# Decoder layer, fp32, one core: where the feed-forward's side work stands in program order

## The chip, the core and the metric

The kernel runs on one core of a Trainium2 chip. The metric is device time in microseconds of one execution. Inside the core, five engines work from queues of their own, each in program order, and meet at semaphores: TensorE (PE; its weight loads are listed as PEld) multiplies matrices, VectorE (DVE) and ScalarE (ACT) work on rows of 128 partitions, GpSimd (POOL) does the same more slowly, SyncE (SP) issues transfers. A profile shows DMA queues (SP's and POOL's are the ones that matter here) whose transfers share 16 DMA engines.

## The reference, cut to what matters

Eight sequences of 256 tokens, width 512, all in float32. One decoder layer with three sublayers, each followed by a layer norm without scale and shift:

```python
x = _layernorm(x + attn(x))                  # 16 heads, low-rank maps folded into the weights
x = _layernorm(x + xattn(x, ctx, ctx, decay))  # q * recurrence over ctx * ctx
gate = jnp.einsum('bsh,ih->bsi', x, gate_w)  # 2048 x 512, a cubic spline through 8134 control points
up   = jnp.einsum('bsh,ih->bsi', x, up_w)
x = _layernorm(x + jnp.einsum('bsi,hi->bsh', silu(gate) * up, down_w))
```

The three weight matrices of the feed-forward are samples of splines, so each row is a smooth curve with few knots. The kernel uses that: it never forms the matrices. It multiplies a 64-row summary of the input for each tile of 128 hidden units.

## The kernel before, in words

Tokens are handled in `NG` = 4 groups of 512, hidden units in `NTILE` = 16 tiles of 128. Attention, the recurrence and the first two norms take the first 400 us of the span; the change does not touch them. What follows is the feed-forward, group by group (`for b in range(NG)`, line 940). One group is:

- *Pairs* (`gate_up`, line 842, for j = 0 to 7). Each pair makes two hidden tiles. The two gates `pg` go to two buffers of the PSUM pool `ps_mm` (4 buffers), the two `pu` to two of `ps_big` (4 buffers); each product uses 64 of the 128 rows of the array, so two run side by side. ACT applies SiLU (`sg`), VectorE multiplies (`inter`).
- *Gathers* (`gather`, line 858). Each `inter` is copied by DMA, 256 KB, into a re-sorted tile `nat`. All 16 gathers are issued on SP.
- *Exact parts* (`exact`, line 865, for t = 0 to 15). Four products of 32 rows each per tile accumulate into the four `y` of the group, which take all four `ps_big` buffers.
- *Sums* (`into_sums`, line 875), four of them, after the eighth exact part. Each multiplies from `nat`, in a `ps_mm` buffer (`ps_s`), is copied to `sum` and moved by DMA into the tile `fin`.
- *Finish* (`finish`, line 894). Four pairs of products from `fin` close the four `y`, and ACT and VectorE copy them to `ys`.

Two other strands are woven in.

*The inputs of the group after* (`inputs(b + 1)`, line 700, run while b is 1 or 2; those of groups 0 and 1 are made during attention). It is a generator of eight units. Units 0 to 3 transpose the normalised rows `x2` (four 128x128 transposes each into a `ps_mm` buffer, `tr_x`), copy them to `x2T` (ACT and VectorE in turn) and write them to DRAM (`xd`: one large transfer on POOL's queue per unit, and from the second unit on a few single rows on SP's). Units 4 to 7 form the *moments*: two products each (`ps_mom`, three `ps_mm` buffers in all); after the second and the last, copies to `mom`, and at the end two writes to DRAM on POOL's queue (`md`). The reads back into `xg` (`windows`, line 683, four transfers behind one more small write; `moments`, line 694, two transfers) are kept in a list `reads` and issued on SP after the last pair.

*The results of the group before* (`outcome(b - 1, t)`, line 907, t = 0 to 3). Four transposes of `ys` into a `ps_mm` buffer (`tr_y`); VectorE adds the residual `x2p` and sums the rows (`h3`, `s3`); then `norm_plain` (line 366): the mean's negative `nm` (VectorE), the square with its row sum (ACT, whose elementwise output goes to `o`), variance and power −1/2 (POOL: `va`, `rs`), the normalised rows (VectorE, to `o`); last the output DMA on SP. `h3` and `o` come from the pool `rows` (6 buffers). A third generator, `residual(b)`, copies `x2` into `x2p` on POOL.

The order of every engine is the program's order: `Ordered` (line 299) pins it. Generators are advanced by two functions. `slot()` (line 348) takes every chain in `chains` one `yield` further; `fill(n)` (line 354) takes n units of the inputs and calls `slot()` after every second one. So the loop at line 940 decides what stands between what: in groups 1 and 2 one unit of the inputs follows each pair, and one more result is begun after each of the first four exact parts. Behind the last group, four results are begun one per `slot()`, and `settle()` runs the chains out.

Of the kernel before, what the change touches and what calls it, by code (L numbers as in the profile page):

```python
# [10 lines left out]
F32 = mybir.dt.float32  # L11
U32 = mybir.dt.uint32
AF = mybir.ActivationFunctionType
# [4 lines left out]
P = 128  # L18
B, T, D = 8, 256, 512
NH, DH = 16, 32  # L20
NT = B * T
DC = D // P
# [4 lines left out]
NG = NT // GT  # L27
TC = GT // P
# [287 lines left out]
def decoder_kernel(ctx: ExitStack, tc: tile.TileContext, x, xT, ctxT, wq, wkT, wvT, woT, wdownT, wup, decay, up_taps, down_taps, mom_f, sum_f, out, plan):  # L316
    nc = tc.nc
# [5 lines left out]
    rows = ctx.enter_context(tc.tile_pool(name="rows", bufs=6, side="left"))  # L323
# [21 lines left out]
    nc = Ordered(tc)  # L345
    units, chains = [], []

    def slot():

        for c in list(chains):  # L350
            if next(c, c) is c:
                chains.remove(c)

    def fill(n):

        for i in range(n):
            if units:
                next(units[0][1])
                units[0][2] -= 1
                if not units[0][2]:  # L360
                    units.pop(0)
            if i % 2:
                slot()
                some_taps()

    def norm_plain(h, s, o):

        nm = small.tile([P, 1], F32, tag="nm", name="nm")
        nc.vector.tensor_scalar(nm, s, -1.0 / D, None, ALU.mult)
        yield  # L370
        ss = small.tile([P, 1], F32, tag="ss", name="ss")
        nc.scalar.activation(o, h, AF.Square, bias=nm, accum_out=ss)
        yield
        va = small.tile([P, 1], F32, tag="va", name="va")
        nc.gpsimd.tensor_scalar(va, ss, 1.0 / D, EPS, ALU.mult, ALU.add)
        rs = small.tile([P, 1], F32, tag="rs", name="rs")
        nc.gpsimd.tensor_tensor(rs, va, neghalf[:, 0:1], ALU.pow)
        yield
        nc.vector.tensor_scalar(o, h, nm, rs, ALU.add, ALU.mult)
# [61 lines left out]
    def some_taps():  # L441
        made[0] += 0.62
        while made[0] >= 1:
            made[0] -= 1
            next(weights, None)
# [237 lines left out]
    def windows(xd, xt, xg):  # L683


        past = SPAN * ND - D
        nc.sync.dma_start(out=xd[4 * (SPAN - past) + 3 :: 4, :], in_=xt[:past, 0, :])
        for h, odd, n, j0 in ((0, 0, NTILE // 2 - 1, 1), (1, NTILE - 1, NTILE // 2 - 1, 0)):
            for t, m, j in ((odd, 1, odd // 2), (2 * j0 + h, n, j0)):
                step = 4 * (lows[t + 2][0] - lows[t][0]) if m > 1 else 0  # L690
                from_ = bass.AP(xd.tensor, xd.offset + 4 * lows[t][0] * GT, [[GT, RAW], [step * GT, m], [1, GT]])
                nc.sync.dma_start(out=xg[h * K2 : h * K2 + RAW, j : j + m, :], in_=from_)

    def moments(md, xg):
        for h in range(2):
            to = h * K2 + RAW
            from_ = bass.AP(md.tensor, md.offset + h * GT, [[NTILE * GT, 20], [2 * GT, NTILE // 2], [1, GT]])
            nc.sync.dma_start(out=xg[to : to + 20], in_=from_)

    def inputs(b):  # L700

        pool, mf = ffn["pool"], ffn["mf"]
        xt = pool.tile([P, DC, GT], F32, tag="x2T", name="x2T")
        xd = ffn["dram"].tile([4 * SPAN, GT], F32, tag="xd", name="xd")
        md = ffn["dram"].tile([1, 20 * NTILE, GT], F32, tag="md", name="md")
        xg = pool.tile([P, NTILE // 2, GT], F32, tag="xg", name="xg", bufs=2)
        xgs[b] = xg
        for c in range(DC):
            tr = ps_mm.tile([P, GT], F32, tag="mm", name="tr_x2")
            for t in range(TC):  # L710
                nc.tensor.transpose(tr[:, t * P : (t + 1) * P], x2[:, b * TC + t, c * P : (c + 1) * P], ident)
            (nc.vector.tensor_copy if c % 2 else nc.scalar.copy)(xt[:, c, :], tr)
            nc.gpsimd.dma_start(out=xd[c : 4 * (P - 1 - c) + c + 1 : 4, :], in_=xt[c:, c, :])
            if c:
                row = 4 * (SPAN - c) + c - 1
                nc.sync.dma_start(out=xd[row : row + 4 * c - 3 : 4, :], in_=xt[:c, c, :])
            yield
        if b > 1:
            reads.append(lambda: windows(xd, xt, xg))
        else:  # L720
            windows(xd, xt, xg)
        mo = ffn["mom"].tile([P, ND, GT], F32, tag="fin", name="mom")
        ps = {}
        for c in range(DC):
            for s in (c, c + 1):
                if s // 2 not in ps:
                    ps[s // 2] = ps_mm.tile([P, GT], F32, tag="mm", name="ps_mom")
                at = slice(s % 2 * K2, (s % 2 + 1) * K2)
                nc.tensor.matmul(
                    ps[s // 2][at, :],  # L730
                    lhsT=mf[:, c, s - c, :],
                    rhs=xt[:, c, :],
                    start=(s == c + 1 or c == 0),
                    stop=(s == c or c == DC - 1),
                )
            if c == 1:
                nc.vector.tensor_copy(mo[:, 0, :], ps[0])
            if c == DC - 1:
                nc.vector.tensor_copy(mo[:, 1, :], ps[1])
                nc.scalar.copy(mo[:K2, 2, :], ps[2][:K2, :])  # L740
                nc.gpsimd.dma_start(out=md[:, : 2 * P].rearrange("h (c p) t -> (h p) c t", p=P), in_=mo[:, :2, :])
                nc.gpsimd.dma_start(out=md[0, 2 * P :], in_=mo[:K2, 2, :])
                if b > 1:
                    reads.append(lambda: moments(md, xg))
                else:
                    moments(md, xg)
            yield
# [4 lines left out]
    for s, (g, bb, quad) in enumerate(steps):  # L752
# [8 lines left out]
        if quad == 0 and n:  # L761
            load_rows(n - 1)
            o = [["o", output(n - 1, qc), DC] for qc in range(2)]
# [43 lines left out]
        if quad % 2:  # L807
            tr = ps_mm.tile([P, 2, T], F32, tag="mm", name="tr_rec")
# [49 lines left out]
    def gather(b, t):  # L858

        g, r = t // NSUM, t % NSUM  # L860
        if not r:
            nats[b, g] = work.tile([P, NSUM, GT], F32, tag=f"nat{g}", name="nat", bufs=1)
        nc.sync.dma_start(out=nats[b, g][r::NSUM], in_=inters[b, t])

    def exact(b, t):

        if t == 0:
            ys[b] = [ps_big.tile([P, GT], F32, tag="big", name=f"y{d}") for d in range(ND)]
        for d in range(ND):
            q = slice(d * 32, (d + 1) * 32)  # L870
            nc.tensor.matmul(
                ys[b][d], lhsT=wd[q, t * P : (t + 1) * P], rhs=inters[b, t][q, :], start=(t == 0), stop=False
            )
# [33 lines left out]
    def outcome(b, t):  # L907

        tr = ps_mm.tile([P, D], F32, tag="mm", name="tr_y")
        for d in range(ND):  # L910
            nc.tensor.transpose(tr[:, d * P : (d + 1) * P], ys[b][:, d, t * P : (t + 1) * P], ident)
        yield
        h3 = rows.tile([P, D], F32, tag="row", name="h3")
        s3 = small.tile([P, 1], F32, tag="s3", name="s3")
        nc.vector.scalar_tensor_tensor(h3, tr, 1.0, xps[b][:, t, :], ALU.mult, ALU.add, accum_out=s3)
        o = rows.tile([P, D], F32, tag="row", name="o")
        yield from norm_plain(h3, s3, o)
        r0 = (b * TC + t) * P
        nc.sync.dma_start(out=out[r0 : r0 + P, :], in_=o)

    def residual(b):

# [17 lines left out]
    for b in range(NG):  # L940
        if 0 < b < NG - 1:
            units.append(["i", inputs(b + 1), 2 * DC])
        for j in range(NTILE // 2):
            gate_up(b, j)
            gather(b, 2 * j)
            gather(b, 2 * j + 1)
            if b:
                slot()
                fill(1)
        if b == 0:  # L950
            fill(2 * DC)
        while reads:
            reads.pop(0)()
        for t in range(NTILE):
            exact(b, t)
            if b and t < TC:
                chains.append(outcome(b - 1, t))
            slot()
            if b == 0 and t < 5:
                slot()  # L960
            if b == 0 and t == 4:
                settle()
                done.close()
                late = ffn["mom"] = ctx.enter_context(tc.tile_pool(name="late", bufs=1, side="right"))
            if t == 7:
                settle()
                chains.append(residual(b))
                for v in range(NSUM // 2):
                    into_sums(b, v)
        assert not units  # L970
        finish(b)
    for t in range(TC):
        chains.append(outcome(NG - 1, t))
        slot()
    settle()
    mid.close()

# [50 lines left out]
```

## Time and profile before

Three runs took 611.3, 610.93 and 611.07 us, median 611.07. The profiled execution took 612.27 us; its span is 610.5 us, and mean granted TensorE clock 0.993 of full speed.

| stage (us from the span's start) | length | PE busy | DVE busy | ACT busy | POOL busy | DMA share |
|---|---|---|---|---|---|---|
| group 1, 449.56 to 501.35 | 51.79 | 50.24 | 20.82 | 16.05 | 14.88 | 0.77 |
| group 2, 501.35 to 555.36 | 54.01 | 51.94 | 20.86 | 16.04 | 14.89 | 0.74 |
| group 3, 555.36 to 598.89 | 43.53 | 43.53 | 18.48 | 14.95 | 11.36 | 0.62 |
| tail, 598.89 to 610.5 | 11.61 | 1.93 | 6.09 | 3.22 | 3.26 | 0.24 |

How to read it: all engines' operations are recorded by one helper (line 308), so groups of instructions are told apart by tile names (`y<-fin` is a product whose operand comes from `fin`). Busy time of TensorE includes the drain of pipelined products. A timeline line gives start, length, engine, operation, output and inputs, shape, count, and in brackets the idle time before it with what ended that. The chain of waits follows the last instruction back to what released it. The DMA share is the mean busy share of the 16 DMA engines, and can read a little over 1. A granted clock of 0.5 means that TensorE ran at half speed.

### The profile page before, as it was taken

How to read it: one execution, taken by the hardware profiler on the slowest of the kernel's cores; microseconds unless marked ns; L12 is line 12 of the kernel's file. 1: busy time of each engine (PE TensorE's matmuls, PEld its weight loads, DVE VectorE, ACT ScalarE, POOL GpSimd, SP SyncE). 2: the span in 40 equal slices, each digit the busy share in tenths (PEclk: the TensorE clock that was granted, in tenths of full speed). 3: DMA queues.
4: the chain of work that ended last, by engine and by line, in shares of the span. 5: the costliest groups of instructions: out<-in, count | busy, mean ns of one | idle time of the engine just before them, and what ended most of it. 6: DMA issues, size and time to landing. Idle time of an engine off the chain costs nothing.

```text
span 610.5 us, 9688 instructions
## 1 busy us (share of the span) xinstructions
PE 584.3 (96%) x3346; PEld 288.8 (47%) x3346; DVE 334.5 (55%) x742; ACT 276.9 (45%) x820; POOL 210.1 (34%) x479
## 2 busy tenths in 40 slices
PE   8999999998999999999999898899999989999993
PEld 3544555555455555555556455444343333334432
DVE  0204545657875666786665778867635316504614
ACT  0115634647555456565556666664233214304402
POOL 0001986264636334644420301202511611350152
PEclk9999999999999999999999999999999999998998
DMA  8104253044124114314101653588129849973931
GB/s 301 52 0 155 89 182 92 20 139 138 53 68 141 35 53 160 118 52 139 47 23 53 176 141 108 156 195 177 71 71 246 226 121 236 222 208 79 217 119 69
DMA packets 39984, 75.50 MB, mean 124 GB/s; under 512 B 3936, under 2 KB 8288, under 8 KB 39936
## 3 DMA queue, kind: packets, MB, share of 16 engines
q1 hardware_dynamic: 36880, 66.94, 40.1%
q0 software_dynamic: 2048, 6.77, 3.4%
q10 hardware_dynamic: 1008, 1.18, 0.6%
q8 instruction: 26, 0.43, 0.3%
q14 instruction: 22, 0.18, 0.1%
HBM read 42.86 MB, written 11.04 MB: 88 GB/s over the span
## 4 chain that ended last, share of the span: by engine, by line
PE 72%; DVE 10%; issue 7%; DMA 5%; ACT 3%; POOL 2%; SPq 0%; POOLq 0%; DVEq 0%; ACTq 0%
PE ps_k L308 9%; PE ps_v L308 9%; PE ps_o L308 8%; PE y L308 8%; PE ps_q L308 7%; PE tr_e L308 6%; PE sc L308 5%; PE av L308 5%; PE pg L308 4%; PE pu L308 3%; DVE nmax L308 3%; PE ps_s L308 2%; DMA xg<-md 2%; ACT e L308 2%; PE ps_mom L308 2%
## 5 line engine op out<-in xcount | busy, mean ns | idle before, releaser
L308 ACT ACTIVATE e<-sc,nmax 128x256 f32<-128x256 f32 x256 | 120.3, 481 | 101.4 <-DVE nmax L308 101.3
L308 DVE TENSOR_REDUCE nmax<-sc 128x2 f32<-128x512 f32 x128 | 84.4, 681 | 73.6 <-PE sc L308 67.6
L308 POOL TENSOR_TENSOR taps<-taps 128x256 f32<-128x256 f32 (+1 forms) x144 | 89.0, 618 | 32.1 <-DMA taps<-in_down_taps 24.2
L308 PE MATMUL tr_e<-ident,e 128*128 128x128 f32 x512 | 68.3, 276 | 0.6 <-DVE eT L308 0.4
L308 PEld LDWEIGHTS tr_e<-ident,e 128*128 128x128 f32 x512 | 56.9, 140 | 25.2 <-issue 22.5
L308 PE MATMUL y<-inter,wd 32*128 32x512 f32 x512 | 63.6, 605 | 0.0
L308 PE MATMUL ps_o<-w_o,yT 128*128 128x512 f32 x128 | 60.0, 600 | 1.9 <-DVE eT L308 1.6
L308 PE MATMUL ps_k<-xT_g,w_k 128*128 128x512 f32 x128 | 58.7, 600 | 0.6 <-DVE eT L308 0.6
L308 PE MATMUL ps_v<-w_v,xT_g 128*128 128x512 f32 x128 | 58.6, 598 | 0.4 <-DVE eT L308 0.4
L308 PE MATMUL ps_q<-xT_g,w_q 128*128 128x512 f32 x128 | 58.2, 596 | 0.0
L308 POOL TENSOR_SCALAR va<-ss 128x1 f32<-128x1 f32 x32 | 7.0, 220 | 144.5 <-ACT x L308 85.8
L308 DVE TENSOR_TENSOR inter<-pu,sg 128x512 f32<-128x512 f32 x64 | 41.2, 686 | 26.6 <-PE pu L308 13.7
L308 ACT ACTIVATION_READ_ACCUMULATOR e<-sc,nmax 128x1 f32 x256 | 53.3, 208 | 0.0
L308 POOL TENSOR_TENSOR rs<-va,neghalf 128x1 f32<-128x1 f32 x48 | 28.0, 584 | 70.3 <-DVE va L308 67.6
L308 ACT ACTIVATE sg<-pg 128x512 f32<-128x512 f32 x64 | 36.1, 596 | 30.1 <-PE pg L308 29.9
L308 DVE COPY eT<-tr_e 128x512 f32<-128x512 f32 x64 | 43.7, 682 | 0.5 <-PE tr_e L308 0.4
L308 PE MATMUL av<-eT,v_g 128*32 128x256 f32 x512 | 36.7, 385 | 5.0 <-ACT eT L308 2.7
L308 PEld LDWEIGHTS y<-inter,wd 32*128 32x128 f32 x512 | 25.2, 184 | 28.9 <-issue 24.4
L308 ACT COPY eT<-tr_e 128x512 f32<-128x512 f32 x64 | 37.5, 586 | 2.4 <-PE tr_e L308 2.4
L308 PE MATMUL sc<-k_g,q_g 32*128 32x256 f32 x512 | 37.4, 401 | 0.2 <-ACT e L308 0.2
L308 POOL TENSOR_TENSOR r<-r 128x1024 f32<-128x1024 f32 x8 | 15.2, 1896 | 63.3 <-DMA r<-in_ctxT 63.3
L308 PEld LDWEIGHTS ps_v<-w_v,xT_g 128*128 128x128 f32 x128 | 23.1, 190 | 25.5 <-issue 24.3
(97 smaller groups left out, 734.0 us busy)
## 6 DMA issues: line engine op xcount, KB each, us to landing
nat<-inter SPq DMA_DIRECT2D x64, 256.0 KB
taps<-in_down_taps SPq DMA_DIRECT2D x40, 256.0 KB
taps<-in_up_taps SPq DMA_DIRECT2D x16, 384.0 KB
xg<-xd SPq DMA_DIRECT2D x8, 616.0 KB
r<-in_ctxT SPq DMA_DIRECT2D x8, 512.0 KB
x_t<-in_x SPq DMA_DIRECT2D x16, 256.0 KB
fin<-sum SPq DMA_DIRECT2D x16, 256.0 KB
out<-o SPq DMA_DIRECT2D x16, 256.0 KB
```

The lines of the kernel that those rows point to most:

```text
L308: return lambda *a, **k: self.tc.keep_in_program_order(f(*a, **k))
```

## The change

Three edits in the loop, one in the results.

- In groups 1 and 2 the four transposing units of the next inputs run in front of the first pair, one behind the other; the four moment units run behind the third pair (j = 2), one behind the other. The reads into `xg` stay behind the last pair. In group 3 there are no units left, and the two calls of `fill` only call `slot()` twice more.
- The four results of the group before are all begun after the first exact part, so `slot()` takes them through their steps together: 16 transposes, four sums, four squares, four pairs on POOL, four normalisations, four output transfers.
- Behind the last group the same: four results at once.
- `norm_plain` gets an argument for where the square's elementwise output goes. For results it is the PSUM tile `tr` that held the transposes, and the rows are normalised in place in `h3`; the tile `o` is gone.

```diff
-    def norm_plain(h, s, o):
+    def norm_plain(h, s, o, other=None):
...
-        nc.scalar.activation(o, h, AF.Square, bias=nm, accum_out=ss)
+        nc.scalar.activation(o if other is None else other, h, AF.Square, bias=nm, accum_out=ss)
...
-        o = rows.tile([P, D], F32, tag="row", name="o")
-        yield from norm_plain(h3, s3, o)
+        yield from norm_plain(h3, s3, h3, tr)
         r0 = (b * TC + t) * P
-        nc.sync.dma_start(out=out[r0 : r0 + P, :], in_=o)
+        nc.sync.dma_start(out=out[r0 : r0 + P, :], in_=h3)
...
         if 0 < b < NG - 1:
             units.append(["i", inputs(b + 1), 2 * DC])
+            fill(DC)
         for j in range(NTILE // 2):
             gate_up(b, j)
             gather(b, 2 * j)
             gather(b, 2 * j + 1)
             if b:
                 slot()
-                fill(1)
+            if b and j == 2:
+                fill(DC)
...
             exact(b, t)
-            if b and t < TC:
-                chains.append(outcome(b - 1, t))
+            if b and t == 0:
+                chains += [outcome(b - 1, c) for c in range(TC)]
             slot()
...
-    for t in range(TC):
-        chains.append(outcome(NG - 1, t))
-        slot()
+    chains += [outcome(NG - 1, t) for t in range(TC)]
     settle()
```

## The prediction

> **What bounds the kernel now.** I read the page first: the engine table and the chain that ended last. TensorE (PE) is busy 96% of the span and carries 72% of the chain, but 5% of it is DMA, and the question is where.
>
> ```profile
> PE 584.3 (96%) x3346; PEld 288.8 (47%) x3346; DVE 334.5 (55%) x742; ACT 276.9 (45%) x820; POOL 210.1 (34%) x479
> PE 72%; DVE 10%; issue 7%; DMA 5%; ACT 3%; POOL 2%; SPq 0%; POOLq 0%; DVEq 0%; ACTq 0%
> ```
>
> The timeline of TensorE shows the four feed-forward groups. S, where a group's first pair begins, is 449.56 for group 1, 501.35 for group 2, 555.36 for group 3. The lines are of group 2, then of group 3 (start, length, what; behind `y<-fin` the idle time before it and what ended it).
>
> ```profile
> 501.35 1.13 PE L308 MATMUL pg<-xg,wg 64*128 64x512 f32 x4
> 502.31 1.02 PE L308 MATMUL pu<-xg,wu 64*128 64x512 f32 x4
> 503.27 0.66 PE L308 MATMUL tr_x<-ident,x 128*128 128x128 f32 x4
> 503.85 1.13 PE L308 MATMUL pg<-xg,wg 64*128 64x512 f32 x4
> ...
> 522.06 1.08 PE L308 MATMUL ps_mom<-x2T,mf 128*64 128x512 f32 x4
> 523.07 1.62 PE L308 MATMUL y<-inter,wd 32*128 32x512 f32 x8
> 524.63 0.66 PE L308 MATMUL tr_y<-ident,ys 128*128 128x128 f32 x4
> 525.21 1.14 PE L308 MATMUL y<-inter,wd 32*128 32x512 f32 x8
> ...
> 533.83 7.09 PE L308 MATMUL ps_s<-nat,sf 128*64 128x512 f32 x32
> 540.85 7.15 PE L308 MATMUL y<-inter,wd 32*128 32x512 f32 x64
> 550.06 5.37 PE L308 MATMUL y<-fin,wd 128*128 128x512 f32 x8 [2.07 <-DMA fin<-sum]
> ...
> 569.30 2.62 PE L308 MATMUL y<-inter,wd 32*128 32x512 f32 x8
> ```
>
> TensorE is unbroken until the last factor `y<-fin`, which waits 2.07 us for a transfer (1.55 in group 1, none in group 3). The chain, queried for group 2, runs through DMA:
>
> ```profile
> 525.15 5.40 DMA md<-mom
> 531.48 13.62 DMA xg<-md
> 545.16 4.76 DMA fin<-sum
> ```
>
> and the table of stages shows the DMA engines full from about S+4 on, and the clock after the wait (columns: window, its length, busy time of PE, PEld, DVE, ACT, POOL, granted clock, DMA share, GB/s):
>
> ```profile
> 500.00:505.00 5.00, 5.00 (x22) 2.14 (x22) 2.41 (x4) 2.26 (x4) 0.16 (x1) 1.00 0.00 0
> 515.00:520.00 5.00, 5.00 (x22) 1.30 (x20) 2.58 (x5) 2.17 (x4) 0.00 (x0) 1.00 1.07 245
> 530.00:535.00 5.00, 5.00 (x41) 2.04 (x41) 2.36 (x6) 1.24 (x4) 3.04 (x11) 1.00 0.85 203
> 551.00:552.00 1.00, 1.00 (x3) 0.48 (x2) 0.00 (x0) 0.59 (x1) 0.00 (x0) 0.50 0.00 0
> ```
>
> So groups 1 and 2 are bound by DMA, narrowly; group 3 and the tail by TensorE and by the norm's chain. The clock was 0.5 from 551.0 to 554.4, and `y<-fin` took 5.37 us there against 3.60 in group 1 (497.75 to 501.35): 1.7 us for a wait of 2.07, nothing for one of 1.55.
>
> **The change, part by part.**
>
> *TensorE, groups 1 and 2.* A pair with four transposes behind it takes 503.85 − 501.35 = 2.50 us. An unbroken pair takes 1.716 (group 3), four transposes 0.43 (13 of `tr_y` in 1.4): each break costs 0.36. A pair with a moment unit takes 2.93 (519.14 to 522.06) against 1.716 + 0.858: 0.36 again. After: 16 transposes 1.72, three pairs 5.15, moments 3.43, five pairs 8.58, some three changes at 0.15 to 0.2: 19.4 instead of 21.72. But the last moments cover VectorE's last two products. Without them the first `y` takes 2.55 us, as in group 3 (569.30 to 571.85), instead of 1.56. Then 16 `tr_y` in one run and three tiles take 4.5 instead of 5.57 us. With four tiles more, `ps_s` starts at about S+30.0 instead of S+32.48, and `y<-fin` is reached at S+44.2 instead of S+46.65. These 2.4 us end in a wait for DMA.
>
> *DMA, groups 1 and 2.* Transfers now move from S+3.95 (the first gather is issued at S+2.79) to S+48.1 (group 1) and S+48.6 (group 2). After: the first transposed block is copied at about S+1.2, POOL issues `xd` at S+1.25 and data move about 1.6 us later, so S+2.85: 1.1 us earlier. By the completion records, the 16 gathers and four `xd` blocks take 23.2 us (505.3 to 528.5); gathers alone run at 1.25 us each in group 3, so `xd` costs 0.8 a block. The moments now end at S+10.7, so the `md` writes (1.6 us of all engines) come before the last gathers, in the stretch where the gathers pause: six gathers are moved by about S+13.5, and the seventh cannot arrive before S+14.8. The gathers end at S+2.85 + 23.2 + 1.6, about S+27.6 (before: 27.15 to 27.54), still ahead of `ps_s`.
>
> Behind them the SP queue has the reads of `xg`, four results and four `fin`. From the last gather to the end of `xg<-md` it is 15.2 us in group 1 and 16.6 in group 2, with the `md` writes inside; without these 13.7 to 15.0. Then results and sums: 4.8 to 5.3. So `fin` lands at about S+47 and `y<-fin` starts at S+47.1, instead of S+48.19 and S+48.71: **−1.1 and −1.6 us**. Bounds: nothing, if start and pause eat it; and −2.4, TensorE's own saving, since the last `fin` is held only until the second `xg<-md` has landed (545.10 before its issue at 545.16).
>
> *Queues and buffers.* On SP the three small `xd` rows move ahead of all gathers; they wait for copies that end by S+2.5, before the first gather can be issued. The stall of SP for `md` (5.0 us in group 1, 1.0 in group 2) goes; next late is the row write at the head of the windows' reads, as before (2.7). On POOL the four `xd` issues (0.55 each) move ahead of nothing else, the two of `md` move before the norm's chains, where POOL sits idle 10.7 us. On ACT and VectorE the copies of the transposes (0.59 and 0.68 each, from S and S+0.75, behind the copies of `y`) come ahead of the first gate; the first pair finds its buffers free by S+1.7, when the transposes end. The fourth pair needs the buffer of the first moments, copied by S+9.7, at S+10.9. The four `tr_y` keep all four `ps_mm` buffers until their squares are written: VectorE's four sums, 0.81 each from S+22.9, end at S+26.2, the last square at S+27.4; `ps_s` asks at S+30.0, so 2.6 us of cover. The results' issues on SP lie behind the reads and are ready by S+28.5; the queue is at them by S+30.
>
> *The clock.* TensorE reaches `y<-fin` 2.4 us earlier and DMA lets it start 1.1 to 1.6 earlier: the waits become about 2.9 us in both groups. Rows: 2.07 us in one window tripped the clock; 1.55, of which 1.36 fell in one of the 3.41 us steps the clock record shows (counted back from 551.0), did not. So 2.9 us most often trips it: I take yes in both, **+1.6 in group 1** (bounds 0 and 1.7), no change in group 2 (bounds −1.7 and 0).
>
> The Trainium skill (TensorE: Matmul & The Clock Gate, "Why this matters for your kernels") says that only gaps above some 3 us, a whole idle window, bring the half clock back. By that rule neither wait would trip it and the +1.6 would fall away; the row of group 2, slowed after 2.07 us, contradicts it and decides.
>
> *Group 3.* Pairs unchanged; four breaks of `tr_y` at 0.36 become one: −1.0, with three tiles and 16 transposes in 4.5 to 4.7 instead of 5.56. `ps_s` would start at 580.1 and need the second half of the gathers 0.9 later, at 581.0; the last landed at 580.73. **−0.9** (bounds −0.3 and −1.1).
>
> *Tail.* Now VectorE's fourth sum waits behind the first normalisation:
>
> ```profile
> 602.84 0.55 DVE L308 TENSOR_SCALAR o<-h,nm,rs 128x512 f32<-128x512 f32 x1 [0.25 <-POOL rs L308]
> 603.49 0.69 DVE L308 SCALAR_TENSOR_TENSOR h<-tr_y,x2p 128x512 f32<-128x512 f32 x1
> 604.92 0.72 ACT L308 ACTIVATE o<-h,nm 128x512 f32<-128x512 f32 x1 [1.43 <-DVE o L308]
> 606.67 0.55 DVE L308 TENSOR_SCALAR o<-h,nm,rs 128x512 f32<-128x512 f32 x1 [1.18 <-POOL rs L308]
> ```
>
> After, it starts at 602.5, its square at 603.5; POOL's powers (0.19 + 0.55 to 0.77 each) then set the pace: the fourth ends at 605.75 instead of 606.64. **−0.9** (bounds −0.4, as POOL's pairs of 0.85 to 1.0 us allow, and −1.0). The square written to PSUM is taken at its 0.72 us.
>
> **Sum** against the profiled execution, 612.27 us (span 610.5): −1.1 − 1.6 + 1.6 − 0.9 − 0.9 = −2.9, so 609.4. The median of the runs is 611.07, 1.2 below that; taking the same difference off, **608.1 us**.
>
> **Rivals.**
>
> *A: at most one wait trips the clock.* For: it depends on where the 3.41 us steps fall. One trip: −2.9 − 1.65 = −4.5, 606.5 us; none: −6.2, 604.9.
>
> *B: the end of DMA does not move.* For: bytes are the same, and the share is over 1.0 for 20 us. Against: nothing moves in S to S+4. Groups 1 and 2 gain 0, the clock trips in both: +1.6 − 1.8 = −0.2, **610.9 us**.
>
> *C: a hole in the DMA feed, slower.* Place: the moments' 3.7 us behind the third pair, when no gather is made. If the early `xd` blocks give nothing (1.1 back) and the pause (S+13.5 to S+14.8) stays empty because `md` is issued after it, `y<-fin` starts at S+49.6 to S+49.9, 1.3 later than now on average: 2.6 + 1.6 − 1.8 = +2.4, **613.5 us**. It decides from gathers ending at S+29.7, where the total is over +1.2. Against: `md` can be issued at S+11.4, when the copies of the moments end.
>
> **How the numbers follow.** Forecast 0.45, A 0.30, B 0.12, C 0.13. A measurement of this kernel tells 0.2% (1.2 us) from no change, so forecast and A are faster, B mostly the same (a quarter of it, with a DMA gain of half, faster), C slower: 0.78, 0.09, 0.13. The range reaches from A without any trip, 604.9 less 0.3 for the sizes, into the lower part of C, 611.8; the forecast's own is 606.5 to 609.6.
>
> **What would show it.** Right: in groups 1 and 2 pairs at 1.72 us, `ps_s` near S+30, last gather near S+27.6, `y<-fin` waiting 2.5 to 3.2 us for `fin<-sum` and starting near S+47; clock 0.5 after it; tail from the last `y<-fin` to the end 0.9 shorter. Wrong: `ps_s` waiting for gathers, DMA share under 0.9 between S+12 and S+16, `y<-fin` later than S+48.5, or a first `y` of more than 2.6 us.

## The result, and the profile after

Four runs of the changed kernel took 614.18 to 616.36 us, median **616.15 us**; the kernel before, run beside it, 611.0 (610.32 to 611.3). The ratio is 1.0079 (95% interval 1.0056 to 1.0101): slower by 0.8%, where 608.1 was forecast and the range ended at 611.8. The profiled execution took 616.05 us with a span of 614.3, 3.8 more than before.

The page's engine table and chain, kernel after:

```profile
PE 582.3 (95%) x3346; PEld 293.8 (48%) x3346; DVE 334.7 (54%) x742; ACT 277.7 (45%) x820; POOL 210.6 (34%) x479
PE 74%; DVE 10%; DMA 9%; ACT 3%; issue 2%; SPq 1%; POOLq 0%; POOL 0%; DVEq 0%; ACTq 0%
```

DMA's share of the chain went from 5% to 9%, some 25 us more of it, although TensorE's work is the same 3346 instructions. The timeline of TensorE shows where (start, length, what, and the wait in brackets). S is now 449.86, 505.42 and 561.00. The first line is of group 1 before the change, the second of group 1 after it, the others of group 2 after it. A product shows as two instructions, so the four products of `y<-fin` are x8; in the text, the length of `y<-fin` runs to the next group's first product, without the drain.

```profile
497.75 3.67 PE L308 MATMUL y<-fin,wd 128*128 128x512 f32 x8 [1.55 <-DMA fin<-sum]
...
499.07 6.51 PE L308 MATMUL y<-fin,wd 128*128 128x512 f32 x8 [4.82 <-DMA fin<-sum]
...
505.42 1.91 PE L308 MATMUL tr_x<-ident,x 128*128 128x128 f32 x16
507.26 1.13 PE L308 MATMUL pg<-xg,wg 64*128 64x512 f32 x4
...
512.61 3.65 PE L308 MATMUL ps_mom<-x2T,mf 128*64 128x512 f32 x16
...
524.98 2.63 PE L308 MATMUL y<-inter,wd 32*128 32x512 f32 x8
527.55 1.97 PE L308 MATMUL tr_y<-ident,ys 128*128 128x128 f32 x16
...
535.66 7.09 PE L308 MATMUL ps_s<-nat,sf 128*64 128x512 f32 x32
542.68 7.15 PE L308 MATMUL y<-inter,wd 32*128 32x512 f32 x64
555.41 5.65 PE L308 MATMUL y<-fin,wd 128*128 128x512 f32 x8 [5.58 <-DMA fin<-sum]
```

TensorE does what the change asks of it: the side work stands in runs, the first `y` takes 2.63 us without its cover, and the last factor is reached 2.3 us earlier, at S+44.4. Then it waits 4.82 and 5.58 us for `fin`, instead of 1.55 and 2.07. The chain of waits in group 2 (start, length, what):

```profile
527.11 7.52 DMA xd<-x2T
...
536.32 14.12 DMA xg<-md
550.50 4.77 DMA fin<-sum
555.41 4.80 PE y L308 x6
```

The reads of `xg` and the results with their sums take about what was expected in this chain (14.1 and 4.8 us); what is late is their beginning. The windows (columns as in the prediction: window, length, busy time of PE, PEld, DVE, ACT, POOL, clock, DMA share, GB/s):

```profile
460.00:465.00 5.00, 5.00 (x24) 2.04 (x22) 2.55 (x4) 2.86 (x5) 1.28 (x2) 1.00 1.07 258
...
499.00:500.00 1.00, 0.93 (x1) 0.50 (x2) 0.00 (x0) 0.00 (x0) 0.00 (x0) 0.50 0.00 0
500.00:505.00 5.00, 5.00 (x8) 2.03 (x7) 0.69 (x1) 1.02 (x2) 0.00 (x0) 0.52 0.00 0
```

From S+10 to S+15 (the first line), where the gathers pause, DMA is full: no hole. And `y<-fin` runs at half clock: the clock's record shows 0.5 for 6.83 us from 497.97 and from 552.59, where before it showed 3.41 us from 551.0, in group 2 alone.

Where the 3.8 us come from, by the starts and ends of TensorE's lines:

| | predicted | measured |
|---|---|---|
| start of group 1 | 0 | +0.3 |
| start of `y<-fin`, group 1 (S+48.19 to S+49.22) | −1.1 | +1.0 |
| start of `y<-fin`, group 2 (S+48.72 to S+49.99) | −1.6 | +1.3 |
| length of `y<-fin`, group 1 (3.60 to 6.35) | +1.6 | +2.75 |
| length of `y<-fin`, group 2 (5.30 to 5.59) | 0 | +0.3 |
| group 3, up to its `y<-fin` | −0.9 | −1.1 |
| tail, from there | −0.9 | −0.8 |
| sum | −2.9 | +3.8 |

Everything but DMA and its clock came about as forecast. The record of the DMA packets shows more, group by group, up to the end of `fin`. *Engine time* is the sum of all packets' durations over 16 engines, *idle* what is left, so that end = start + engine time + idle; packets can overlap a little (shares above 1), so idle is a remainder and not a measured pause. The last column counts SP's packets of 2 KB that took under 100 ns. All times in us behind S:

| group | start | engine time (SP's queue) | idle | end | SP packets under 100 ns, up to S+27 |
|---|---|---|---|---|---|
| before, 1 | 4.00 | 39.82 (34.33) | 4.24 | 48.05 | 633 |
| before, 2 | 4.01 | 40.16 (34.49) | 4.40 | 48.58 | 588 |
| after, 1 | 2.51 | 42.26 (36.60) | 4.31 | 49.07 | 245 |
| after, 2 | 2.52 | 42.35 (36.61) | 4.99 | 49.86 | 273 |

Transfers begin 1.5 us earlier and the idle time changes little (+0.1 and +0.6), but *the same bytes cost 2.2 to 2.4 us more engine time*, nearly all of it on SP's queue (2.3 and 2.1). The DMA view over the first 27.64 us of group 1 shows the same on fewer numbers. Kernel before, then kernel after (queue: packets, MB, share of 16 engines; issues: count, KB, median us to landing):

```profile
q1 hardware_dynamic: 2417, 4.38, 68.4%
q0 software_dynamic: 470, 1.58, 18.0%
...
md<-mom POOLq DMA_DIRECT2D x1, 512.0 KB, 6.4
...
xd<-x2T POOLq DMA_DIRECT2D x1, 254.0 KB, 4.5
```

```profile
q1 hardware_dynamic: 2304, 4.20, 72.9%
q0 software_dynamic: 512, 1.69, 19.9%
...
md<-mom POOLq DMA_DIRECT2D x1, 512.0 KB, 3.7
xd<-x2T POOLq DMA_DIRECT2D x1, 256.0 KB, 2.4
xd<-x2T POOLq DMA_DIRECT2D x1, 254.0 KB, 3.3
```

SP's queue (q1) moved less in more time: 0.684 × 27.64 / 4.38 = 4.32 us per MB before, 0.729 × 27.64 / 4.20 = 4.80 after. POOL's queue (q0) is hardly dearer (3.15 and 3.25 us per MB), and its transfers land sooner.

### The profile page after: what moved, and what is told of

Same layout as the page of the kernel before. It is cut to its first block, busy times and chain, and to the rows that moved or that the text cites. A ratio compares the mean times of both kernels' runs of the same rounds, so it can differ in the third digit from the quotient of the medians.

```text
span 614.3 us, 9693 instructions
## 1 busy us (share of the span) xinstructions
PE 582.3 (95%) x3346; PEld 293.8 (48%) x3346; DVE 334.7 (54%) x742; ACT 277.7 (45%) x820; POOL 210.6 (34%) x479
## 3 DMA queue, kind: packets, MB, share of 16 engines
q0 software_dynamic: 2048, 6.77, 3.4%
## 4 chain that ended last, share of the span: by engine, by line
PE 74%; DVE 10%; DMA 9%; ACT 3%; issue 2%; SPq 1%; POOLq 0%; POOL 0%; DVEq 0%; ACTq 0%
PE ps_k L308 9%; PE ps_v L308 9%; PE y L308 8%; PE ps_o L308 8%; PE ps_q L308 7%; PE tr_e L308 6%; PE sc L308 5%; PE pg L308 5%; PE av L308 5%; DMA xg<-md 4%; PE pu L308 4%; DVE nmax L308 3%; DMA xd<-x2T 2%; PE ps_s L308 2%; PE ps_mom L308 2%; ACT e L308 2%
## 5 line engine op out<-in xcount | busy, mean ns | idle before, releaser
L308 DVE TENSOR_TENSOR inter<-pu,sg 128x512 f32<-128x512 f32 x64 | 41.2, 686 | 18.3 <-PE pu L308 12.4
L308 ACT ACTIVATE sg<-pg 128x512 f32<-128x512 f32 x64 | 37.3, 597 | 18.4 <-PE pg L308 18.4
L308 PEld LDWEIGHTS y<-inter,wd 32*128 32x128 f32 x512 | 26.7, 184 | 32.7 <-issue 26.9
```

The source lines that it names most:

```text
L308: return lambda *a, **k: self.tc.keep_in_program_order(f(*a, **k))
```

## Experiments

Two theories stood after the result. *Mixing*: a packet of the gathers costs less when it alternates with packets of POOL's `xd` and `md` (about 84 ns for its 2 KB in such stretches, about 160 ns where gathers follow gathers); the change pulls the two apart in time, so the gathers lose the cheap packets. In group 3, where POOL moves nothing, the first 2048 packets of SP's queue, almost all of them gathers, took 160 ns on average in both kernels. *Place*: it is merely when transfers are put in the queue, or some part of the change other than the inputs. Besides: how much is the clock?

### One part at a time

**The results alone** (four at once and in place, inputs as before):

```diff
-            if b and t < TC:
-                chains.append(outcome(b - 1, t))
+            if b and t == 0:
+                chains += [outcome(b - 1, c) for c in range(TC)]
...
-        yield from norm_plain(h3, s3, o)
+        yield from norm_plain(h3, s3, h3, tr)
```

> The kernel before with the results' part alone: four results at once, normalised in place; the inputs' units stay one behind each pair. All theories: group 3 about 1.1 us shorter, the tail 0.75 shorter, as in the changed kernel. In groups 1 and 2 the transfers keep their order, so `y<-fin` still starts at about S+48.2 and S+48.7 while TensorE is there 0.9 us earlier; waits 2.4 and 2.9 us. If the longer wait in group 1 does not trip the clock: 609.2 us; if it trips it: 610.9 to 611.9 us.

Measured 612.66 us, ratio 1.0003 (0.9986 to 1.0019): no change. Group 3 and the tail gain as in the full change (38.70 us to the last factor instead of 39.79, 14.57 us from there instead of 15.35). But in group 1 TensorE reaches `y<-fin` 1.1 us earlier (S+45.55), DMA ends 0.4 earlier (47.60), and the longer wait trips the clock. Timeline of TensorE, results alone:

```profile
498.33 5.37 PE L308 MATMUL y<-fin,wd 128*128 128x512 f32 x8 [2.19 <-DMA fin<-sum]
```

2.19 us of wait, 5.30 us for the products of `y<-fin` instead of 3.60: the 1.7 us eat the gain.

**The inputs alone:**

```diff
             units.append(["i", inputs(b + 1), 2 * DC])
+            fill(DC)
...
                 slot()
-                fill(1)
+            if b and j == 2:
+                fill(DC)
```

> The kernel before with the inputs' part alone: transposes in front of the first pair, moments behind the third; results as before. Both theories of the DMA (mixing: a gather is cheap only while POOL's queue has packets to alternate with; hole: the gathers pause under the moments and the engines starve) put the whole loss here: `y<-fin` at S+49 to S+50, clock 0.5 behind both waits, 617 to 618.5 us. If it were the results' part that lost, this would be at or below 611.

Measured 616.83 us, ratio 1.0078 (1.0051 to 1.0105), the whole of the loss; waits of 3.65 and 4.35 us, `y<-fin` 6.46 and 5.30 us. Engine time 41.82 and 42.28 us, 280 and 336 cheap packets. The loss sits in the inputs.

**The transposes in front alone** (moments as before, behind pairs 5 to 8):

```diff
+            fill(DC)
...
-                fill(1)
+                if j >= DC:
+                    fill(1)
```

> The kernel before with only the transposes in front of the first pair; moments one unit behind each of pairs 5 to 8, results as before. Mixing: the xd blocks (some 250 packets of POOL's queue) go out ahead of the gathers, so as many gather packets lose some 77 ns: SP's queue 34.4 + 1.2 = 35.6 us of engine time a group; transfers begin 1.1 us earlier, so `y<-fin` stays near S+48.5. TensorE is there at S+45.5, the wait of 3 us trips the clock in both groups: 612 to 613.5 us. Rival, the moments' run alone does the harm: engine time 34.4, `y<-fin` at S+47.2, about 610.

**The moments in one run alone** (behind the fourth pair; transposes as before):

```diff
-                fill(1)
+                if j < DC:
+                    fill(DC + 1 if j == DC - 1 else 1)
```

> The kernel before with only the moments in one run (behind the fourth pair, since the transposes stay one behind each of the first four). Mixing: the md writes (some 160 packets) fall into the pause: SP's queue 34.4 + 0.8 = 35.2 us, `y<-fin` near S+49, waits of 2.5 to 3 us with the clock tripped: 613 to 614.5 us. Rival, the transposes alone do the harm: engine time 34.4, `y<-fin` at S+48.2 to S+48.7 as before, 611 to 612.

| | time, ratio | engine time | start, end of DMA (group 1; group 2) | TensorE at `y<-fin` |
|---|---|---|---|---|
| transposes | 613.47, 1.0043 (1.0025 to 1.0061) | 41.81; 41.44 | 2.51, 48.12; 2.51, 48.19 | S+45.3 |
| moments | 618.19, 1.012 (1.0097 to 1.0143) | 40.60; 41.32 | 4.01, 49.19; 4.03, 50.22 | S+46.6 |

The transposes cost 2.0 and 1.3 us of engine time (138 and 166 cheap packets are left) and win 1.5 back by starting earlier, so DMA ends where it did; TensorE is earlier, and its wait of 2.9 us trips the clock in both groups (5.2 and 5.3 us). The moments' run costs 0.8 to 1.2 us of engine time and about 0.4 of idle, and gives TensorE nothing, which I had not seen. Timeline of TensorE, moments alone:

```profile
460.06 3.65 PE L308 MATMUL ps_mom<-x2T,mf 128*64 128x512 f32 x16
...
470.71 2.62 PE L308 MATMUL y<-inter,wd 32*128 32x512 f32 x8
...
499.37 5.37 PE L308 MATMUL y<-fin,wd 128*128 128x512 f32 x8 [2.73 <-DMA fin<-sum]
```

What the run saves in breaks between pairs, the uncovered first `y` (2.6 instead of 1.6 us) takes back.

The two parts cost in different places. The first 2048 packets of SP's queue took 18.0 and 18.4 us of engine time before the change; with the transposes in front they take 20.4 and 20.3, with the moments' run 18.3 and 18.4. So the transposes make the gathers dearer. The moments' run leaves them nearly alone; its cost lies in POOL's own packets (+0.4 and +0.2 us) and in SP's packets behind the gathers (+0.1 and +0.9), and no run shows why. The two parts together cost less (1.0078) than the sum of their ratios: in both together the moments stand a pair earlier, but whether that is why was not tried.

### What the clock takes

Full change, with five products more ahead of `finish` in groups 1 and 2, so that TensorE is not idle while it waits (x10 in the timeline, two instructions each):

```diff
         assert not units
+        if 0 < b < NG - 1:
+            idle_ps = ps_mm.tile([P, GT], F32, tag="mm", name="ps_idle")
+            for _ in range(5):
+                nc.tensor.matmul(idle_ps, lhsT=wd[:, :P], rhs=nats[b, 0][:, 0, :], start=True, stop=True)
         finish(b)
```

> The changed kernel with five idle products of 128x512 on TensorE between the last exact part and `y<-fin` in groups 1 and 2 (4.3 us into a PSUM buffer that nobody reads). It prices the clock alone: the transfers end where they ended (S+49.2 and S+50.0), but TensorE is not idle before. If the half clock is a matter of the wait: `y<-fin` takes 3.6 us instead of 6.35 and 5.6, no 0.5 in the clock record between 450 and 600 us, 4.7 us less than the changed kernel, about 611.4. If the clock falls for another reason: 616.

Measured 611.06 us, ratio 0.9993 (0.9978 to 1.0008): level with the kernel before. Timeline of TensorE:

```profile
494.03 4.56 PE L308 MATMUL ps_idle<-nat,wd 128*128 128x512 f32 x10
498.98 3.67 PE L308 MATMUL y<-fin,wd 128*128 128x512 f32 x8 [0.39 <-DMA fin<-sum]
...
546.82 4.56 PE L308 MATMUL ps_idle<-nat,wd 128*128 128x512 f32 x10
551.99 3.67 PE L308 MATMUL y<-fin,wd 128*128 128x512 f32 x8 [0.61 <-DMA fin<-sum]
```

DMA is as late as in the full change (`y<-fin` at S+49.27 and S+49.51), yet it takes 3.5 to 3.6 us, and the half clock is gone from the record up to the tail. So 5.1 us of the changed kernel's time are the clock's answer to the idle time. They are not all new: 1.7 of them stood in group 2 before.

The Trainium skill (TensorE: Matmul & The Clock Gate, "Why this matters for your kernels") lets a gap go unpunished up to some 3 us. The runs here disagree: 0.56, 1.11 and 1.55 us passed, but 2.07, 2.19, 2.30 and 2.34 us each brought a step at half clock, and about 1.7 us. The length alone does not settle how many steps: with the inputs alone, 3.65 us brought two and 4.35 us one.

### Why the gathers are dearer

**Later issue.** The full change, with the issues of `xd` (behind pairs 1 to 4) and `md` (behind pair 8) moved back in program order:

```diff
+            if b > 1:
+                writes.append(spread)
+            else:
+                spread()
...
+            if writes and (j < 4 or j == 7):
+                writes.pop(0)()
```

> The changed kernel, but the transfers that the inputs issue (xd blocks and rows, md) are issued where they were before: behind pairs 1 to 4 and behind the last; transposes and moments stay in their runs, so the pause in the gathers stays and md no longer fills it. Mixing: DMA engine time of a group falls from 42.3 back to about 40 us (share times time), the last gather lands by S+27.5, `y<-fin` starts near S+48; about 613 us. Hole: the pause is now emptier, the last gather lands at S+30 or later, `y<-fin` at S+50, 617 us or more.

Measured 615.86 us, ratio 1.0055 (1.0033 to 1.0077). It did not do what it was to do. POOL is idle there, so each issue goes out as soon as its data are ready, wherever it stands in the program: `xd` still went at S+1.5 to S+3.2 and `md` at S+11.9; only SP's small rows moved. Engine time stayed at 42.16 and 42.11. It tests neither theory.

**Held issue.** So POOL was given something to wait for: a one-column copy of an `inter` of the pair just made, ahead of the second to fourth `xd` block and of `md`.

```diff
+            if writes and j in (0, 1, 2, 4):
+                hold = small.tile([P, 1], F32, tag="hold", name="hold")
+                nc.gpsimd.tensor_copy(hold, inters[b, 2 * j + 1][:, 0:1])
+                writes.pop(0)()
```

> The changed kernel with POOL held back: before the second, third and fourth `xd` block it copies one column of the products of pairs 1, 2 and 3, before `md` one of pair 5, so these transfers go out among the gathers again instead of ahead of them and in their pause. (In the run with spread issues they did not move: POOL is idle there, and a transfer goes as soon as its data are ready.) Mixing: packets of SP's queue under 100 ns before S+27 rise from some 250 to 500 or more of 2000, and the queue's engine time falls from 36.6 to about 35 us a group. Hole, or a fixed price of the packets: 36.6 as before. The end of the transfers says less, since the engines now stand idle after the first block; `y<-fin` at S+48.5 to S+50.

Measured 616.95 us, ratio 1.0081 (1.0053 to 1.0109): the time did not move, the engine time did. The DMA view, held, over the first 27.64 us of group 1:

```profile
q1 hardware_dynamic: 2252, 4.11, 58.6%
q0 software_dynamic: 512, 1.69, 20.8%
```

0.586 × 27.64 / 4.11 = 3.94 us per MB on SP's queue, against 4.80 in the full change and 4.32 before; 848 and 1000 cheap packets; engine time over the group 38.56 and 38.92. That the engines had less to do is not the reason. The DMA views of three microseconds each (held from S+11.0; full change from S+9.0; full change from S+44.3, where results and `fin` move):

```profile
q1 hardware_dynamic: 338, 0.62, 59.1%
q0 software_dynamic: 105, 0.31, 37.5%
...
q1 hardware_dynamic: 350, 0.64, 107.6%
...
q1 hardware_dynamic: 467, 0.85, 74.7%
```

Held, the engines are as good as full (0.97), yet about as many bytes of gathers cost little more than half of what they cost in the full change: 269 of 303 packets of 2 KB took under 100 ns, against none of 312. So putting POOL's transfers among the gathers makes the gathers cheap. But POOL's packets are not needed for a cheap packet: in the last line 409 of 416 took under 100 ns, 85 ns on average, with nothing of POOL's queue beside them. What makes gathers dear to each other was not found.

The windows show what the holding costs (held, then the full change; columns as above):

```profile
452.03:459.53 7.50, 7.50 (x38) 2.87 (x36) 4.70 (x8) 3.44 (x6) 2.13 (x6) 1.00 0.60 176
459.53:467.03 7.50, 7.50 (x36) 3.19 (x34) 4.47 (x7) 4.46 (x8) 1.48 (x3) 1.00 0.91 261
```

```profile
452.36:459.86 7.50, 7.50 (x38) 2.86 (x36) 4.69 (x8) 3.44 (x6) 1.24 (x3) 1.00 0.95 259
459.86:467.36 7.50, 7.50 (x36) 3.20 (x34) 4.48 (x7) 4.47 (x8) 1.28 (x2) 1.00 1.03 244
```

With `xd` held back there is too little to move from S+2.5 to S+10 (share 0.60 instead of 0.95). Idle time rises to 8.45 and 9.37 us, and `y<-fin` starts at S+49.67 and S+50.95. In this kernel packets were mixed and cheap, or early and dear, and the two balance.

**Gathers on two queues.** If it were enough that two queues have work, gathers divided over SP and POOL would be cheap throughout:

```diff
-        nc.sync.dma_start(out=nats[b, g][r::NSUM], in_=inters[b, t])
+        (nc.gpsimd if t % 2 else nc.sync).dma_start(out=nats[b, g][r::NSUM], in_=inters[b, t])
```

> The changed kernel with every second gather issued on POOL's queue. Mixing, if it is a matter of two queues: packets of gathers at about 84 ns instead of 160, all gathers landed by about S+24, `y<-fin` without a wait near S+44.5 to S+46, no half clock; 601 to 604 us. Mixing, if it is a matter of kinds (a gather beside a DRAM write, not beside a gather): packets stay at 160 ns, nothing moves, 616 us. Hole: as the pause stays, no more than 0.5 us, 615.5 us.

Measured 616.65 us, ratio 1.0078 (1.0054 to 1.0102). Engine time fell, to 40.37 and 40.60, but idle rose to 5.76 and 5.72, and `y<-fin` starts at S+48.79 and S+48.97, the wait still past what the clock forgives. POOL's packets are of 4 KB, about 255 ns each, SP's 140 on average: nothing near 84. So it is not any second queue that makes a gather's packet cheap, and why a packet of `xd` or `md` does stays open.

### What is queued ahead of the late transfer

In all these runs the four `fin` stand on SP's queue behind 14 us of reads of `xg`, which nobody needs before the next group. The full change, with `fin` on POOL's queue:

```diff
-        nc.sync.dma_start(out=sorted_[b][v::ND], in_=o)
+        nc.gpsimd.dma_start(out=sorted_[b][v::ND], in_=o)
```

> The changed kernel with the four `fin<-sum` transfers of every group issued on POOL's queue instead of SP's. Theory: `y<-fin` waits only because `fin` stands behind the reads of `xg` and the results in SP's queue; from POOL's queue it alternates with them and lands before TensorE is there at S+44.4. Then groups 1 and 2 take 48.0 us each instead of 55.6, the clock stays, 616.15 - 15.2 = 601 us. Rival, the DMA engines themselves are the limit: `fin` lands at S+47 or later whatever its queue, or the next group's first pair waits as long for `xg`; 612 us or more.

Measured **603.03 us, ratio 0.9862** (0.9837 to 0.9887), the best of all. Timeline of TensorE:

```profile
479.94 7.09 PE L308 MATMUL ps_s<-nat,sf 128*64 128x512 f32 x32
486.95 7.15 PE L308 MATMUL y<-inter,wd 32*128 32x512 f32 x64
494.67 3.67 PE L308 MATMUL y<-fin,wd 128*128 128x512 f32 x8 [0.56 <-issue]
...
543.68 3.67 PE L308 MATMUL y<-fin,wd 128*128 128x512 f32 x8 [1.11 <-DMA fin<-sum]
```

`fin` lands at S+44.87 and S+45.36 instead of S+49.07 and S+49.86; the waits are too short to trip the clock; groups 1 and 2 take 48.47 and 49.10 us. What `fin` passes is not much: in group 1, 0.42 of the 10.14 MB move behind it, beside `y<-fin`; at the full change's 4.2 us per MB that is an estimated 1.8 of the 4.2 us. Up to the end of `fin` the engine time is 40.20 us (42.26 in the full change) and the idle time 2.15 (4.31). Why the idle time falls was not tested. That `fin` gets past reads issued before it agrees with the Trainium skill (DMA: Bandwidth & Descriptors, "Queues, rings and completion order"), by which each DMA engine takes packets from its queues in turn.

**The same edit on the kernel before:**

> The kernel before with the same move of `fin<-sum` to POOL's queue. Theory: groups 1 and 2 take 46.65 + 3.6 = 50.25 us, 1.5 and 3.8 less than now; 605.7 us. Beside the run with both, it says what the change is worth on TensorE once no transfer is waited for: 2.2 us in each of groups 1 and 2, 1.1 in group 3, 0.75 in the tail, about 6 us in all, hidden in the change as it stands. Rival: as in the run with both, 611 us.

Measured 609.65 us, ratio 0.9975 (0.9963 to 0.9987), 4 us short of what I expected. Timeline of TensorE, group 1:

```profile
497.19 3.67 PE L308 MATMUL y<-fin,wd 128*128 128x512 f32 x8 [1.04 <-DMA fin<-sum]
```

`fin` lands at S+47.59 and S+47.99, only half a microsecond earlier, and what is won is mostly group 2's clock (51.73 us instead of 54.01). The last `fin` is issued at S+40.6 and takes 7.0 and 7.4 us to land; in the run above it is issued at S+38.3 and takes 6.5 and 7.0. So on a queue without the reads ahead of it, the change brings the last `fin` forward: it is issued 2.3 us earlier and lands 2.7 and 2.6 us earlier. On SP's queue it landed 1.0 and 1.3 us later. Run beside the one above, it prices the change itself where `fin` does not queue behind the reads: 603.03 − 609.65 = **−6.6 us**. The same edits are worth +5 us with one order of the queue and −6.6 with the other.

**Reads in two pieces.** The kernel of 603.03 us, with each read of 44 rows of `xd` issued as 32 and 12:

```diff
+                for a, n_ in ((0, 32), (32, RAW - 32)):
+                    from_ = bass.AP(xd.tensor, xd.offset + (4 * lows[t][0] + a) * GT, [[GT, n_], [step * GT, m], [1, GT]])
```

> The changed kernel with `fin` on POOL's queue, and each of the four reads of 44 rows into `xg` split into 32 and 12 rows. The reads' completions came from 11 of 16 engines; 32 rows can use 16 and 12 rows 12, so the busiest engines move 21 packets instead of 28 for each large read. If those engines hold `fin` back, the remaining waits (0.6 and 1.1 us) go and the time is 601 to 602 us; if the alternation with other packets holds it, 603 as without the split.

Measured 608.25 us, ratio 0.9955 (0.9935 to 0.9975): 5 us worse than unsplit. Engine time up to the end of `fin` rose to 43.86 and 44.38 (from 40.20 and 40.56), for nearly the same bytes (9.77 MB in group 1, against 9.72). Idle time fell to 0.2 and 0.3 us, so `fin` landed 1.7 and 1.9 us later; the waits of 2.30 and 2.96 us tripped the clock. Timeline of TensorE, group 1:

```profile
496.63 5.37 PE L308 MATMUL y<-fin,wd 128*128 128x512 f32 x8 [2.30 <-DMA fin<-sum]
```

My expectation fell, and the cause of the rise was not found.

**Without the moments' run.** The kernel of 603.03 us, with the moments behind pairs 5 to 8 as before:

```diff
-            if b and j == 2:
-                fill(DC)
+                if j >= DC:
+                    fill(1)
```

> The changed kernel with `fin` on POOL's queue, and the moments put back one unit behind each of pairs 5 to 8 (transposes in front and results at once stay). The run with the moments' part alone reached `y<-fin` no earlier than before (S+46.6) and made the transfers end later. So theory: TensorE is at `y<-fin` at about S+44.3 as with the moments in one run (45.33 of the transposes' part alone, less 1.1 for the results), the md writes alternate with gathers again, `fin` lands no later than S+45, and the time is that of the changed kernel with `fin` on POOL's queue or up to 1.5 us below it: ratio to the kernel before 0.983 to 0.987. If the moments' run was worth something on TensorE: S+45.3 or later, ratio above 0.988.

Measured 604.47 us, ratio 0.9888 (0.9867 to 0.9908), as good as with the run or a little worse. TensorE reaches `y<-fin` at S+44.24, no later than with it, so the run is worth nothing there, as the moments alone had shown. The half on DMA fell: in group 2 `fin` came at S+46.44, and the timeline of TensorE has

```profile
545.31 5.37 PE L308 MATMUL y<-fin,wd 128*128 128x512 f32 x8 [2.34 <-DMA fin<-sum]
```

again a wait just over 2 us, and 1.7 us for it.

## Why the prediction was wrong, point by point

**The bound: right.** Groups 1 and 2 were bound by DMA, group 3 by TensorE, and TensorE's saving did end in a wait.

**TensorE's part: right in sum.** `ps_s` at S+30.2 (S+30.0 forecast), the last factor at S+44.4 (S+44.2). But the saving is the transposes' and the results'; the moments' run contributes nothing, as the first `y` takes back what the saved breaks give.

**DMA: wrong, and this sets the sign.** The step that failed is "The gathers end at S+2.85 + 23.2 + 1.6, about S+27.6". They ended at S+30.04 and S+29.23. The start was pessimistic (S+2.5), and `md` did go into the gathers' pause. What failed is the premise under the whole sum, that the work of the DMA engines stays the same when its order changes. Up to the end of `fin` it grew by 2.4 and 2.2 us. Of that, 1.9 and 1.2 us lie in SP's first 2048 packets, almost all gathers: 18.0 and 18.4 us before, where gathers and `xd` alternate, 19.9 and 19.6 after. Another 0.4 and 0.9 lie in SP's packets behind them. The step's own terms hid this. Its 23.2 us already held 130 and 110 of `md`'s 160 packets of 4 KB, which it added once more and took off again behind the gathers; by the end of `fin` that cancels, and what is left is a lost discount put at nothing. That the gathers ended 2.4 and 1.6 us later than the step says is for the most part the reads: some 180 and 130 of their packets, about 1.8 and 1.4 us, had moved by then. In group 1: −1.5 (start) + 2.4 (engine time) + 0.1 (idle) = +1.0, where −1.1 was forecast; in group 2 −1.5 + 2.2 + 0.6 = +1.3, where −1.6 was. The bounds, nothing and −2.4, had no value on the side of a loss: the bytes stayed the same, the engine time did not. Some 350 fewer cheap packets, at 160 − 84 = 76 ns each over 16 engines, come to an estimated 1.7 us. That order sets the gathers' price was shown by holding POOL back, and the run with the transposes alone shows that it is they who raise it. Why the packets behind the gathers cost more stays open.

Behind the gathers the forecast was right in group 1 and 0.8 us short in group 2: reads 14.0 and 15.8 us (13.7 to 15.0 forecast), results and sums 5.0 and 4.8 (4.8 to 5.3).

**The clock: right that it trips in both groups, wrong in size.** A trip was priced at 1.6, from a wait of 2.07 us. Waits of 4.82 and 5.58 us brought two steps at half clock, and `y<-fin` took 2.75 and 2.0 us over its 3.60: +2.75 in group 1 instead of +1.6.

**Group 3 and tail: right**, −1.1 and −0.8 against −0.9 and −0.9. In the timeline of VectorE after, the last two normalisations wait 0.44 us for POOL's powers, which set the pace as forecast (start, length, what):

```profile
607.85 1.17 DVE L308 TENSOR_SCALAR h<-h,nm,rs 128x512 f32<-128x512 f32 x2
609.46 0.55 DVE L308 TENSOR_SCALAR h<-h,nm,rs 128x512 f32<-128x512 f32 x1 [0.44 <-POOL rs L308]
610.44 0.55 DVE L308 TENSOR_SCALAR h<-h,nm,rs 128x512 f32<-128x512 f32 x1 [0.44 <-POOL rs L308]
```

**The rivals.** A (fewer trips) and B (the end of DMA does not move) fell. C came nearest, 613.5 against 616.15, by luck: it had the sign, and its point of decision (gathers past S+29.7) was met in group 1. Its mechanism fell: the pause was filled and the early blocks did start early. C's hole appeared only in the experiment that held POOL back.

## What to carry to other kernels

Before moving a transfer's producer, do not add up DMA times taken from a stretch where queues overlapped: sum the packets' durations per queue, alone and side by side, and bound the move on both sides. Look at what is queued ahead of the transfer that TensorE waits for: here another queue for four transfers of 256 KB each took 1.5 us off the kernel before and 13 off the changed one, and turned the change from a loss of 0.8% into a part of a gain of 1.4%. And count a wait of TensorE by what it does to the clock as well as by its length: in these runs every wait of 2.07 us or more made `y<-fin` 1.6 to 3.1 us longer.

## What the runs showed of the hardware that was not expected

- 2 KB packets of the gathers took about 160 ns in a row, and many of them about 84 ns where they alternated with POOL's `xd` and `md` packets; POOL's own 4 KB packets took about 210 ns in both kernels. Dividing the gathers between the queues did not do it (140 and 255 ns). Packets of 2 KB of the results and of `fin`, on the same queue as the gathers, took 85 ns with nothing of POOL's beside them.
- TensorE idle for 1.55 us kept its clock; idle for 2.07 and 2.19 us it then ran 3.41 us at half clock, and after 4.82 and 5.58 us 6.83 us. In between, 3.65 us brought 6.83 us and 4.35 us brought 3.41.
- Reads of 44 rows split into 32 and 12 raised the engine time of a group by 3.7 and 3.8 us and cost 5 us.
- A transfer issued by an engine that is idle goes when its data are ready: moving the issue of `md` from behind the third pair to behind the eighth in program order left it at S+11.9.
